# Layer 3 of a four-layer network: the four products that norm a chunk's tokens, spread over the slot schedule

## The chip, the cores and the metric

The kernel runs on one core of one Trainium2 chip. The metric is the device time of one execution in microseconds; the median over several executions is compared. The engines are TensorE (PE), VectorE (DVE), ScalarE (ACT), GpSimd (POOL) and SyncE (SP), which here issues nearly all DMAs.

## The reference

Four layers work in turn on an image batch of shape 8 x 64 x 64 x 64 in float32. The change touches the last layer, a bidirectional selective scan (Mamba) over the time axis and then over the frequency axis. Cut to what matters:

```python
def rms_norm(x, w):
    return x * lax.rsqrt(jnp.mean(x * x, axis=-1, keepdims=True) + EPS) * w

def mamba1(x, nw, ipw, cw, cb, xpw, dtw, dtb, Alog, Dp, opw):
    xn = rms_norm(x, nw)                       # the step that the change is about
    xc, z = split(xn @ ipw.T)
    xc = silu(causal_dwconv(xc, cw, cb))
    dt, Bm, Cm = from(xc @ xpw.T)              # dt = softplus(... )
    # h = h * exp(dt*A) + (dt*xc) * B ;  y = sum over 16 states of h * C
    y = selective_scan(xc, dt, Bm, Cm, -exp(Alog)) + Dp * xc
    return (y * silu(z)) @ opw.T

# time axis: directions 0 and 1; then frequency axis: directions 2 and 3
xt = mamba_bidir(xt, P, 0, 1) @ tlin_w + tlin_b + xt
xf = mamba_bidir(xf, P, 2, 3) @ flin_w + flin_b + xf
```

## The kernel before

**Stages, chunks, steps, slots.** `l3_stage` runs twice, once for each axis. A stage is 16 chunks of 2048 tokens (64 channels each). A chunk is eight steps: four groups `g` of 512 tokens, each in two directions `k` (0 forward, 1 backward). In this document the steps of a chunk are numbered 0 to 7, so odd steps are backward ones. A step works on tiles of 128 x 1024 and takes 16 slots, one for each state `n`. `stream` runs 2048 slots a stage, in one loop over `i`; the order of the program in a slot is the order in which each engine gets its instructions, since everything stands under a manual schedule.

**What a slot does.** For slot `i`, in this order:
- SP: `fetch(i+6)` loads the B and C rows of the state, broadcast to 128 partitions (line 1966, tile `bc`, 8 buffers). The load waits for the buffer that it goes into.
- POOL: `multiply_b(i+3)` makes `hb` (line 465, 4 buffers); and, if slot `i-1` is a *shared* one, `multiply_c(i-1)` on POOL (line 495, tile `h`). Shared slots are n = 1, 4, 7, 10, 13 in even steps and n = 2, 6, 10, 14 in odd ones.
- PE: `gather(i-2)` adds a state's `hc` (or `h`) into the step's sum `acc` (line 287). At n = 2 of a step the first gather of the new step comes after the slot's scan, and ahead of it stands `drain`.
- One piece of the next step's `prepare`, and one call of `advance` (below).
- DVE: `scan(i)` (line 481); `drain` of the step before, at n = 2 (line 1975, `z<-acc,z`: it reads the finished sum from PE); then `multiply_c(i)` on DVE (line 495, tile `hc`), unless the slot is shared.
- ACT: `decay(i+2)` (line 472, tile `dA`).

**The side work.** `begin(c+1)`, which fetches and norms the next chunk's tokens, is a generator in the queue `behind`; `finish`, which projects a finished group and adds the residual, is one in the queue `urgent`. `advance` runs one piece a slot. `urgent` goes first: while a `finish` is pending, and waits for a calm slot or for room in PSUM, nothing of `behind` moves. A `yield` of `CALM` or `CALM_FREE` makes the next piece wait for a slot in which neither it nor the one after is shared.

**begin**, in pieces: load of `raw`; squares on ACT, a mean on PE, `ms` to the small tile `rs` by DMA (twice); the root on ACT (line 1860); the reciprocal on DVE (line 1862); `rs` to a row in HBM (line 1865); two broadcasts of that row into `inv` (line 1869, 512 KB each, in pieces of 64 values); then four products `xn = raw * inv` on POOL (line 1877, 128 x 560 each), which `prepare` of the next chunk's steps reads. Counting the pieces through `advance` for a chunk in the middle of a stage gives these places, written (step, n): root (3, 3), reciprocal (3, 4), row (3, 5), `inv` (3, 7), the products (3, 9), (3, 10), (3, 11), (3, 12). A `finish` of two steps earlier holds `urgent` from n = 3 to n = 14 of every even step. The next chunk's first `prepare` starts at (7, 1).

`begin` stands beside the stream 15 times in each stage, 30 times in all; the first chunk's `begin` runs alone ahead of each stage.

Of the kernel before, what the change touches and what calls it, by code (L numbers as in the profile page):

```python
# [249 lines left out]
class Net:  # L250
# [1518 lines left out]
    def l3_stage(self, s, src, dst):  # L1769
# [6 lines left out]
        with ExitStack() as ctx:  # L1776
# [56 lines left out]
            def begin(c):  # L1833

                b, part = divmod(c, 2)
                q, rows = b // 2, slice((b % 2) * C, (b % 2) * C + C)
                x = raw[c % 2]
                hold = chunks[c] = {"x": x}
                from_ = src[q, rows, part * 4 * W : (part + 1) * 4 * W].rearrange("p (s t) -> p s t", t=HW)
                for r in range(2):  # L1840
                    nc.sync.dma_start(x[r * C : r * C + C, :, ends[r]], from_)
                yield False
                yield False
                rs = p1.tile([128, 16], F32, name="rs")
                for j in range(2):
                    yield CALM_FREE
                    sq = p1.tile([C, T], F32, name="sq")
                    o = sq.rearrange("p (s t) -> p s t", t=HW)
                    nc.scalar.activation(o, x[:C, j * 2 * H : (j + 1) * 2 * H, ends[0]], AF.Square)
                    yield  # L1850
                    ps = pp.tile([128, T], F32, name="mm")
                    self.mm(ps[:1, :], mean, sq)
                    yield CALM
                    ms = p1.tile([1, T], F32, name="ms")
                    nc.scalar.copy(ms, ps[:1, :])
                    yield False
                    nc.sync.dma_start(rs[j * 64 : j * 64 + 64], ms.rearrange("o (p e) -> o p e", e=16))
                yield False
                yield CALM_FREE
                nc.scalar.activation(rs, rs, AF.Sqrt, bias=self.eps5)  # L1860
                yield False
                nc.vector.reciprocal(rs, rs)
                yield False
                row = hp.tile([1, 4 * W], F32, name="rs")
                nc.sync.dma_start(row.rearrange("o (p e) -> (o p) e", e=16), rs)
                yield False
                yield False
                for r in range(2):
                    nc.sync.dma_start(
                        inv[r * C : r * C + C, :, ends[r]], row.rearrange("o (s t) -> o s t", t=HW).to_broadcast([C, 4 * H, HW])  # L1870
                    )
                yield False
                yield False
                hold["xn"] = p2.tile([128, 4 * H, HW + 6], F32, name="xn")
                for g in range(4):
                    at = slice(g * H, g * H + H)
                    nc.gpsimd.tensor_tensor(hold["xn"][:, at], x[:, at], inv[:, at], ALU.mult)  # L1877
                    yield False

            behind = deque()  # L1880
            begun = {}
# [2 lines left out]
            class Step:  # L1884
# [93 lines left out]
                def done(self):  # L1978
                    c, g = self.c, self.g
                    if self.k == 1:  # L1980
                        net.urgent.append(Task(finish(c, g, [chunks[c]["y0"], chunks[c]["y1"]])))
                    if self.k == 0 and g == 0 and c + 1 < 2 * NB:
                        begun[c + 1] = Task(begin(c + 1))
                        behind.append(begun[c + 1])
# [29 lines left out]
            with tc.manual_schedule():  # L2014
                Task(begin(0)).run()
                steps = [Step(c, g, k) for c in range(2 * NB) for g in range(4) for k in range(2)]
                self.stream(pools, (6, 3, 6), steps, behind)
# [26 lines left out]
```

## Time and profile before

| what | value |
|---|---|
| median of 3 runs | 25221.08 us |
| lowest, highest | 25216.33, 25233.35 us |
| the profiled execution | 25231.76 us |
| its span, first to last instruction | 25229.9 us |
| slots of layer 3, first to last scan | 11806 to 18470 us and 18547 to 25215 us |
| mean granted TensorE clock | 0.930 |

The span stands on the profile's page; the times of instructions are counted from its start. The profiled execution is 10.7 us longer than the median. Layer 3's two streams are 13332 us of the span, 53%. A line of the timeline has the start (us), the duration (us), engine, line, operation, tiles (out<-in), shape, count, and in brackets the idle time of the engine before it with what ended it.

### The profile page before, as it was taken

To read this page: it belongs to the slowest core of one execution; us is meant where nothing else is said; L and a number is where in the kernel's file an instruction comes from. 1 tells how busy PE (TensorE), PEld (TensorE's weight loads), DVE (VectorE), ACT (ScalarE), POOL (GpSimd) and SP (SyncE) were. 2 spreads that over 40 slices of the span, in tenths; PEclk is the share of its full clock that TensorE was granted. 3 is DMA by queue.
4 is the path that set the end of the run, shared out by engine and by line. 5 is a ranking of instruction groups with operands and counts; after the bars stand their busy time and mean duration, and the time that the engine had idled before them with its cause. 6 is when DMAs were issued, how large, how long until landed. Compare 5 with 4: busy or idle time off the path is not lost. (4 is left out here: it accounts for less than half of the span.)

```text
span 25229.9 us, 193412 instructions
## 1 busy us (share of the span) xinstructions
PE 21360.9 (85%) x53146; PEld 8333.8 (33%) x53146; DVE 22529.7 (89%) x13020; ACT 14745.3 (58%) x18562; POOL 22031.7 (87%) x10775
## 2 busy tenths in 40 slices
PE   8777888888888888888888888888878888888888
PEld 5522333333333323322333333333323333333333
DVE  4379989989989769978999999999989999999999
ACT  4344555555555455524666666666656666666666
POOL 0089999999999759976999999999989999999999
PEclk9888999999999999989999999999989999999999
DMA  2279898889898758842555555555545555555554
GB/s 60 77 279 321 310 317 311 311 313 316 307 315 311 251 194 323 324 134 79 167 170 169 171 166 171 169 170 167 167 155 169 168 170 168 170 168 171 167 171 157
DMA packets 1772400, 5282.72 MB, mean 209 GB/s; under 512 B 536352, under 2 KB 542564, under 8 KB 1703472
## 3 DMA queue, kind: packets, MB, share of 16 engines
q1 hardware_dynamic: 1744176, 5207.00, 61.0%
q10 hardware_dynamic: 27136, 63.34, 0.8%
q8 instruction: 423, 6.93, 0.1%
q14 instruction: 665, 5.45, 0.1%
HBM read 5112.85 MB, written 156.11 MB: 209 GB/s over the span
## 5 line engine op out<-in xcount | busy, mean ns | idle before, releaser
L465 POOL TENSOR_TENSOR hb<-du,bc 128x1024 f32<-128x1024 f32 x4608 | 10749.6, 2357 | 495.7 <-DVE h L481 334.4
L287 PE MATMUL acc<-hc,ident 128*128 128x512 f32 x18816 | 8878.8, 613 | 85.8 <-DVE img L1228 55.9
L472 ACT ACTIVATE dA<-dt,w_A 128x512 f32<-128x512 f32 x8192 | 5662.8, 691 | 4111.9 <-DVE hc L495 3125.9
L481 DVE TENSOR_TENSOR_SCAN dA<-dA,hb 128x1024 f32<-128x1024 f32 x3384 | 7726.0, 2283 | 282.5 <-ACT dA L472 118.4
L287 PE MATMUL acc<-h,ident 128*128 128x512 f32 x7808 | 4553.3, 713 | 2368.4 <-POOL h L495 2368.3
L287 PEld LDWEIGHTS acc<-hc,ident 128*128 128x128 f32 x18816 | 3689.4, 200 | 5292.2 <-issue 4656.8
L465 POOL TENSOR_TENSOR hb<-du,b 128x1024 f32<-128x1024 f32 x2048 | 4869.0, 2402 | 495.0 <-DVE h L481 253.7
L495 DVE TENSOR_TENSOR hc<-dA,bc 128x1024 f32<-128x1024 f32 x3296 | 4034.2, 1224 | 260.8 <-issue 8.9
L472 ACT ACTIVATE dA<-dt,w_l_A 128x1024 f32<-128x1024 f32 x2560 | 2856.5, 1117 | 1187.5 <-DVE hc L495 761.8
L481 DVE TENSOR_TENSOR_SCAN dA<-dA,carry,hb 128x1024 f32<-128x1024 f32 x1320 | 3093.9, 2344 | 172.9 <-ACT carry L1211 111.0
L287 PEld LDWEIGHTS acc<-h,ident 128*128 128x128 f32 x7808 | 1546.1, 215 | 5028.1 <-POOL h L495 3162.1
L481 DVE TENSOR_TENSOR_SCAN h<-dA,hb 128x1024 f32<-128x1024 f32 x1352 | 3081.5, 2279 | 46.0 <-ACT dA L472 40.3
L495 POOL TENSOR_TENSOR h<-h,bc 128x1024 f32<-128x1024 f32 x1312 | 3090.1, 2355 | 14.2 <-DVE h L481 14.2
L495 DVE TENSOR_TENSOR hc<-dA,c 128x1024 f32<-128x1024 f32 x1408 | 1722.5, 1223 | 115.6 <-DMA c<-bc 4.6
L495 POOL TENSOR_TENSOR h<-h,c 128x1024 f32<-128x1024 f32 x640 | 1511.9, 2362 | 8.6 <-ACT carry L1211 8.1
L481 DVE TENSOR_TENSOR_SCAN h<-dA,carry,hb 128x1024 f32<-128x1024 f32 x600 | 1404.4, 2341 | 77.9 <-ACT dA L472 71.6
L472 ACT ACT_TABLE_LOAD x1122 | 1439.5, 1283 | 21.1 <-ACT tmp L997 1.2
L1211 ACT COPY carry<-dA 128x1 f32<-128x1 f32 x1056 | 167.9, 159 | 1735.9 <-DVE hc L495 1674.0
L1911 PE MATMUL mm<-xn,taps 128*128 128x512 f32 x2048 | 937.9, 600 | 34.6 <-POOL xn L1877 32.3
L694 POOL MEMSET xf<- 128x24 f32 x33 | 4.3, 142 | 910.7 <-PE ps L715 731.3
L1926 PE MATMUL mm<-u,w_xp 128*36 128x512 f32 x1024 | 519.1, 632 | 140.5 <-ACT u L1923 135.4
L1946 POOL TENSOR_TENSOR du<-dt,u 128x1024 f32<-128x1024 f32 x256 | 601.4, 2349 | 18.7 <-ACT dt L396 18.7
(310 smaller groups left out, 18613.5 us busy)
## 6 DMA issues: line engine op xcount, KB each, us to landing
bc<-bc SPq DMA_DIRECT2D x4096, 512.0 KB
b<-bc SPq DMA_DIRECT2D x2048, 512.0 KB
c<-bc SPq DMA_DIRECT2D x2048, 512.0 KB
bc<-bc SPq DMA_DIRECT2D x512, 1024.0 KB
tmp<-rs SPq DMA_DIRECT2D x93, 512.0 KB
raw<-x SPq DMA_DIRECT2D x64, 512.0 KB
inv<-rs SPq DMA_DIRECT2D x64, 512.0 KB
tmp<-x SPq DMA_DIRECT2D x192, 128.0 KB
```

The lines of the kernel that those rows point to most:

```text
L287: self.nc.tensor.matmul(o, lhsT, r, start=start, stop=stop)
L465: nc.gpsimd.tensor_tensor(s.shaped(hb[i]), s.shaped(s.du), B.pop(i), ALU.mult)
L472: nc.scalar.activation(dA[i][:, cut], s.dt[:, cut], AF.Exp, scale=A[:, n : n + 1])
L481: nc.vector.tensor_tensor_scan(h[:, way], dA[i][:, way], hb.pop(i)[:, way], s.first(n), ALU.mult, ALU.add)
L495: engine.tensor_tensor(s.shaped(o), s.shaped(h), CC.pop(i), ALU.mult)
L694: nc.gpsimd.memset(x[:, :, HW:], 0.0)
L1211: nc.scalar.copy(self.carry[:, n : n + 1], h[:, last : last + 1])
L1911: nc.tensor.matmul(tokens(px[:, j * W : j * W + W]), taps[k][:, m, j * 128 : j * 128 + 128], xn[:, :, f : f + HW], start=m == 0, stop=m == 1,)
L1926: nc.tensor.matmul(pd, xp[:, k, j, :], u[:, j * W : j * W + W], start=j == 0, stop=j == 1)
L1946: nc.gpsimd.tensor_tensor(du, dt, u, ALU.mult)
```

## The change

One more empty piece stands between the root and the reciprocal, and eight more empty pieces stand between one product and the next. An empty piece costs one call of `advance`. Nothing else is changed.

```diff
                 nc.scalar.activation(rs, rs, AF.Sqrt, bias=self.eps5)
                 yield False
+                yield False
                 nc.vector.reciprocal(rs, rs)
                 yield False
                 row = hp.tile([1, 4 * W], F32, name="rs")
...
                 for g in range(4):
                     at = slice(g * H, g * H + H)
                     nc.gpsimd.tensor_tensor(hold["xn"][:, at], x[:, at], inv[:, at], ALU.mult)
-                    yield False
+
+                    for _ in range(9 if g < 3 else 1):
+                        yield False
```

Counted through `advance` in the same way, the places become: reciprocal (3, 5), row (3, 6), `inv` (3, 8), the products (3, 10), (4, 14), (5, 7), (6, 0). The gaps between the products are 20, 9 and 9 slots: the first gap holds the slots in which a pending `finish` keeps `behind` from moving.

## The prediction

> **What bounds the kernel now.** I read the waits of VectorE in layer 3 first (engine, line, what it waited for, total us, times, longest):
>
> ```profile
> DVE z L1975 <- PE acc L287: 159.1, 43, 5.6
> DVE dA L481 <- ACT dA L472: 70.7, 12, 34.0
> DVE rs L1862 <- ACT rs L1860: 49.4, 31, 16.7
> ...
> DVE dA L481 <- POOL hb L465: 4.8, 9, 2.0
> ```
>
> In the streams VectorE is nearly always running: the 70.7 us are mostly the starts of the stages. So a VectorE wait in a stream is time of the kernel, and two lines are left: the drain (L1975) and the reciprocal. Of the 159.1 us, by the rows of L1975, 144.1 us fall on the drain of step 3, in each of the 30 chunks with side work: 3.9 to 5.6 us, mean 4.81. The other drains wait 15 us in all. The windows of the two streams show a second engine as full (us, PE, PEld, DVE, ACT, POOL busy):
>
> ```profile
> 11806.00:18470.00 6664.00, 5723.76 (x11984) 2174.60 (x11982) 6446.78 (x3661) 4467.50 (x5772) 6457.36 (x2936) 0.95 0.52 168
> ```
>
> GpSimd is at 97%, with little to catch up with. The timeline of one chunk (GpSimd) shows the burst in step 3, the first and last of the four products, and the shared product n = 14 that closes the step, late:
>
> ```profile
> 14072.94 2.34 POOL L495 TENSOR_TENSOR h<-h,bc 128x1024 f32<-128x1024 f32 x1
> 14075.24 2.35 POOL L465 TENSOR_TENSOR hb<-du,bc 128x1024 f32<-128x1024 f32 x1
> 14077.55 2.34 POOL L1946 TENSOR_TENSOR du<-dt,u 128x1024 f32<-128x1024 f32 x1
> ...
> 14080.05 2.36 POOL L465 TENSOR_TENSOR hb<-du,bc 128x1024 f32<-128x1024 f32 x1
> 14082.45 1.37 POOL L1877 TENSOR_TENSOR xn<-raw,inv 128x560 f32<-128x560 f32 x1
> ...
> 14095.65 1.38 POOL L1877 TENSOR_TENSOR xn<-raw,inv 128x560 f32<-128x560 f32 x1
> ...
> 14103.90 2.36 POOL L495 TENSOR_TENSOR h<-h,bc 128x1024 f32<-128x1024 f32 x1
> ```
>
> TensorE and VectorE behind it, in the same chunk, then TensorE at the ends of steps 5 and 7 for comparison:
>
> ```profile
> 14106.32 3.78 PE L287 MATMUL acc<-h,ident 128*128 128x512 f32 x4 [4.51 <-POOL h L495]
> 14109.89 2.41 PE L287 MATMUL acc<-hc,ident 128*128 128x512 f32 x4
> ```
>
> ```profile
> 14061.17 0.25 DVE L1862 RECIPROCAL rs<-rs 128x16 f32<-128x16 f32 x1 [1.09 <-ACT rs L1860]
> ...
> 14112.33 1.23 DVE L1975 TENSOR_TENSOR z<-acc,z 128x1024 f32<-128x1024 f32 x1 [4.89 <-PE acc L287]
> ```
>
> ```profile
> 14208.61 2.51 PE L287 MATMUL acc<-h,ident 128*128 128x512 f32 x4 [3.23 <-POOL h L495]
> 14210.91 3.09 PE L287 MATMUL acc<-hc,ident 128*128 128x512 f32 x4
> ```
>
> ```profile
> 14311.16 1.98 PE L287 MATMUL acc<-h,ident 128*128 128x512 f32 x4 [1.50 <-POOL h L495]
> 14312.98 1.88 PE L287 MATMUL acc<-hc,ident 128*128 128x512 f32 x4
> ```
>
> The chain is: shared product 14 on GpSimd, eight matmuls, drain. In odd steps without a burst that product ends 6.54 us before VectorE is ready to drain (median of steps 5 and 7). The eight matmuls need 3.75 us after it when TensorE waited briefly, 5.45 in the slower of those steps, and 6.03 (median) in step 3. The burst makes the product 4 x 1.33 = 5.3 us later (1.33 is the pitch, 14082.45 to 14083.78). Then 6.03 + 5.3 - 6.54 = 4.8 us, the wait that is seen. Nothing of the 5.3 is caught up between, since GpSimd's idle gaps in odd steps lie at n = 5 to 7; from n = 8 on there is none.
>
> **The change part by part.**
>
> *The reciprocal, one slot later.* VectorE waits 1.09 us for the root, in each chunk (32.7 us over 30). A slot of 3.5 us more covers it. But the root and two table loads also delay ScalarE: the decay for the slot after is done at 14063.86, and the next scan, moved up by 1.09 from 14064.75, would want it at 14063.66. It waits some 0.2. Gain 0.9 us a chunk; between 0 and 1.1.
>
> *The row and the broadcast, one slot later on SP's queue.* This is the part that costs. SP works in order:
>
> ```profile
> 14066.20 0.35 SPq L1865 DMA_DIRECT2D rs<-rs  x1
> 14066.66 2.04 SPq L1966 DMA_DIRECT2D bc<-bc  x2
> 14069.89 4.65 SPq L1869 DMA_DIRECT2D inv<-rs  x2
> 14075.31 31.78 SPq L1966 DMA_DIRECT2D bc<-bc  x11
> ```
>
> The load at 14075.31 is slot 8's, and it waits for the buffer that shared product n = 6 on GpSimd frees (14072.94 + 2.34 = 14075.28). In the trace slot 8 of odd steps waits so in nearly every chunk. Now `inv` is issued ahead of that load; after the change it stands behind it, so not 3.5 us later but 5.8: at 14075.28 + 0.42 = 14075.70. The first product needs `inv`: from that product's end to it GpSimd has two `hb` more, a `du` and, with the slot added, a third `hb`: 9.5 us, so it is due at 14084.75. From the issue of `inv` to the start of its first reader the trace has 12.5 to 14.5 us in the seven chunks with a marked wait, and in the others last packet plus the 1.5 us that those show: 10 to 12.6, median of all about 11.5. One load ahead of it instead of two takes off perhaps 0.5; I take 11. GpSimd then waits 0.42 + 11 - 9.5 = 1.9 us in the first product's slot, where before the median wait is nil. The ends are 0 and 5.4 (at 14.5). Queued behind it are three `hb` and shared products 10 and 14, and TensorE's sums behind those.
>
> *Product 1, alone at (3, 10).* Product 14 of step 3 is later by 1.33 + 1.9 = 3.2 us instead of 5.3. TensorE's wait before it stays long, so 6.03 us is the nearest row for the matmuls: drain wait 6.03 + 3.2 - 6.54 = 2.7, and with rounding 2.8. Gain 2.0 us a chunk. With no wait for `inv` it would be 5.45 + 1.33 - 6.54 = 0.25, with 5.4 it would be 6.3.
>
> *Product 2 at (4, 14).* In slot 14 it comes behind shared product 13, the last of its step, so no drain stands behind it. Its 1.33 us is taken up by step 5's idle, 0.63 + 1.19 us before n = 6 and 7. Cost 0; without that cover it would be added to product 3.
>
> *Product 3 at (5, 7)* comes behind that idle and is not caught up: product 14 of step 5 is 1.33 us later. Its drain has 6.54 - 1.33 = 5.2 us for the matmuls: nothing lost at 3.75, 0.25 at 5.45, 0.8 at 6.03. TensorE's wait there, 1.3 to 3.2 us now, becomes 2.7 to 4.5, so rather the slow rows: 0.4. The Trainium skill, "TensorE: Matmul & The Clock Gate", section "What's actually happening", has the array fall to half clock after about 3.4 us of idle; the row with 3.23 us of idle above is already partly slow, so by the trace the limit lies somewhat lower. By the page half of these drains would stay quick and the sum would be some 6 us better.
>
> *Product 4 at (6, 0)* is behind step 5's last shared product. With what product 3 left and 0.67 us of idle in step 6, GpSimd is 2.0 us late at that step's end; the drain has 8.9 us from product 13 on and needs 5.5 to 7.1. Cost 0.1, up to 0.6. Step 7 has 2.1 us of idle for the rest. The first `prepare` that reads the products starts at (7, 1), 17 slots later.
>
> *The empty pieces* cost nothing on an engine, and `begin` ends long before the next chunk needs it.
>
> **The sum**, a chunk: 2.0 (drain 3) + 0.9 (reciprocal) - 0.4 (drain 5) - 0.1 (drain 6) = 2.4 us; times 30 = 72 us. The profiled execution of 25231.76 would be 25160; it lies 10.7 above the median, so 25149, 0.29% below 25221.
>
> **The rivals.** *A, the broadcast is in time.* If slot 8's load gets a buffer that VectorE frees, or the broadcast takes under 9.1 us with fewer loads beside it, drain 3 waits 0.25: (4.56 + 0.9 - 0.5) x 30 = 149 us, 25072. For it: packets alone take 7 to 10 us. Against: nearly all chunks show that buffer, and no broadcast was readable earlier than about 10 us.
>
> *B, a new wait for the old one.* The broadcast takes about 13.4 us, as in the chunks with a marked wait. GpSimd waits 4.3 us, drain 3 waits 5.2, and 4.81 - 5.2 + 0.9 - 0.5 = 0: 25221. For it: those seven rows. Against: they had two loads ahead.
>
> *C, slower.* Same place, but the broadcast loses its bandwidth to the loads of slots 8 to 11, which now follow it or go with it rather than being held. From 13.4 us it costs time; from 15.1 us (1.67 us a chunk more, 50 us) it can be measured; at 16.5 it is 3.1 x 30 = 93 us, 25314. Against: the longest of 30 is 14.5, and the bc loads are just as dense there.
>
> *D, the spread doesn't come about as counted*: product 2 directly nine slots on, at (4, 3). It would fall ahead of step 4's idle, 0.4 to 0.7 us, and change the sum by under 10 us; it is inside the forecast.
>
> **How the numbers follow.** Some 0.2%, 50 us, is what a measurement of this kernel tells from no change. Forecast with D 0.50, of which 0.10 gains under 50 us (broadcast over 11.8 us); A 0.20; B 0.20; C 0.10. Faster 0.40 + 0.20, same 0.10 + 0.20, slower 0.10. The range goes from A, 25070, to just above B, 25225, and leaves out C and the tail of A.
>
> **What would show it.** In the profile after: L1877 first in step 3, with a GpSimd wait for `inv` of about 2 us in most chunks (some 60 us in all; none would be A, over 120 B or C); SP's `inv` right behind a `bc` load that waited for POOL L495; the reciprocal's wait gone; drain waits of about 2.8 us at step 3 and 0 to 0.8 at step 5. A drain wait over 1 us at step 5 or 6, or a scan that waits for `hb`, would prove the lag arithmetic wrong.

## The result, and the profile after

| | before | after |
|---|---|---|
| median of 5 runs | 25221.08 us | 25129.41 us |
| lowest, highest | 25213.87, 25233.35 us | 25125.93, 25136.76 us |
| ratio, 95% interval | | 0.9963 [0.9951, 0.9975] |
| profiled execution | 25231.76 us | 25126.08 us |
| layer 3's streams, first to last scan | 6664.2 + 6668.4 us | 6623.3 + 6621.0 us |

The median fell by 92 us, 0.36%; 72 were forecast, and 25129 lies inside the range of 25070 to 25225. The streams of layer 3 are 88.3 us shorter. (The profiled executions differ by 105.7 us; the other 17.4 lie ahead of layer 3's first scan, where nothing was changed: that point falls between 11788.7 and 11807.4 us in the ten profiles of this study.)

VectorE's waits in layer 3, after (what waited, for what, total us, times, longest):

```profile
DVE z L1978 <- PE acc L287: 58.7, 73, 3.9
DVE h L481 <- ACT dA L472: 43.8, 55, 0.8
DVE dA L481 <- ACT dA L472: 40.6, 32, 31.9
DVE rs L1863 <- ACT rs L1860: 17.1, 1, 17.1
```

The drains (now L1978) wait 58.7 us instead of 159.1; the reciprocal no longer waits in a stream (the 17.1 us are one wait ahead of the second stage). The second line is new: it had 2.9 us before.

GpSimd in the same chunk of the first stage as was shown before, from shared product 6 of step 3 to shared product 14:

```profile
14042.95 2.35 POOL L495 TENSOR_TENSOR h<-h,bc 128x1024 f32<-128x1024 f32 x1
...
14050.08 4.68 POOL L465 TENSOR_TENSOR hb<-du,bc 128x1024 f32<-128x1024 f32 x2
14056.13 1.37 POOL L1878 TENSOR_TENSOR xn<-raw,inv 128x560 f32<-128x560 f32 x1 [1.37 <-DMA inv<-rs]
...
14071.29 2.36 POOL L495 TENSOR_TENSOR h<-h,bc 128x1024 f32<-128x1024 f32 x1
```

SP's queue there:

```profile
14038.40 7.25 SPq L1969 DMA_DIRECT2D bc<-bc  x2
14045.74 3.23 SPq L1870 DMA_DIRECT2D inv<-rs  x2
```

The broadcast stands behind the load that shared product 6 releases: that product ends at 14045.30, `inv` is issued at 14045.74, the first product is due at 14054.76 and starts at 14056.13, 10.4 us after the issue. Over layer 3 GpSimd's waits for `inv` are these, after:

```profile
POOL xn L1878 <- DMA inv<-rs: 95.5, 31, 40.0
```

One of the 31 is the 40.0 us ahead of the second stage; the other 30, one in each chunk, are 55.5 us, 1.85 each. Before, the 30 chunks had 6.0 in all.

TensorE at the end of step 3, which had 6.03 us of matmuls before:

```profile
14073.71 1.98 PE L287 MATMUL acc<-h,ident 128*128 128x512 f32 x4 [2.56 <-POOL h L495]
14075.53 1.88 PE L287 MATMUL acc<-hc,ident 128*128 128x512 f32 x4
```

Both groups are quick now, 3.7 us together, and this chunk's drain follows at 14077.44 without a marked wait. Over the 30 chunks the drain of step 3 waits 0.59 us instead of 4.80.

The new wait, in step 7 of the same chunk; TensorE, then ScalarE, then VectorE:

```profile
14226.12 3.59 PE L287 MATMUL acc<-h,ident 128*128 128x512 f32 x4 [3.48 <-POOL h L495]
14229.50 3.73 PE L287 MATMUL acc<-hc,ident 128*128 128x512 f32 x8
14233.07 3.67 PE L1914 MATMUL mm<-xn,taps 128*128 128x512 f32 x8
```

```profile
14236.77 1.26 ACT L1926 ACTIVATE u<-mm,w_cb 128x512 f32<-128x512 f32 x2 [1.99 <-PE mm L1914]
...
14243.76 0.58 ACT L1932 COPY dbl<-mm 36x512 f32<-36x512 f32 x1 [2.99 <-PE mm L1929]
14244.24 2.75 ACT L472 ACTIVATE dA<-dt,w_A 128x512 f32<-128x512 f32 x4
```

```profile
14233.27 1.23 DVE L1978 TENSOR_TENSOR z<-acc,z 128x1024 f32<-128x1024 f32 x1 [1.24 <-PE acc L287]
...
14245.75 2.29 DVE L481 TENSOR_TENSOR_SCAN h<-dA,hb 128x1024 f32<-128x1024 f32 x1 [0.81 <-ACT dA L472]
```

Shared product 13 of step 6 is late. Its sums hold the drain (1.24 us) and, on TensorE's queue, the first matmuls of the next `prepare` (L1914). So `u` is late on ScalarE, and so are the matmuls of `dbl` and its copy; on ScalarE's queue the decay stands behind that copy, and the scan at (7, 6) waits 0.81 us for it. A scan eight slots on in the schedule pays for a GpSimd product that it does not read.

### The profile page after: what moved, and what is told of

Read it like the earlier page. It is cut to its first block, busy times and chain, and to the rows that moved or that the text cites. A ratio compares the mean times of both kernels' runs of the same rounds, so it can differ in the third digit from the quotient of the medians.

```text
span 25124.3 us, 193472 instructions
## 1 busy us (share of the span) xinstructions
PE 21234.8 (85%) x53146; PEld 8296.4 (33%) x53146; DVE 22526.0 (90%) x13020; ACT 14730.3 (59%) x18562; POOL 22026.1 (88%) x10775
## 5 line engine op out<-in xcount | busy, mean ns | idle before, releaser
L1914 PE MATMUL mm<-xn,taps 128*128 128x512 f32 x2048 | 937.3, 599 | 34.5 <-POOL xn L1878 32.3
```

What stands on the lines that cost most here:

```text
L1914: nc.tensor.matmul(tokens(px[:, j * W : j * W + W]), taps[k][:, m, j * 128 : j * 128 + 128], xn[:, :, f : f + HW], start=m == 0, stop=m == 1,)
```

## The experiments

All kernels below are edits of the changed kernel, but for the one before idle time without the root slot, which is an edit of the kernel before. T and R in the expectations are the theory and its rival. Each was timed in five rounds against the kernel before, whose medians were 25224.31 us in the first four and 25223.44 us in the last four comparisons. The intervals reach some 0.12% (30 us) to either side; differences between these kernels that are smaller rest on the spread of the runs, 8 to 28 us from lowest to highest, and on the waits in the profiles.

| kernel | places of reciprocal, `inv`, products | median us | ratio, 95% interval |
|---|---|---|---|
| changed | (3,5), (3,8); (3,10), (4,14), (5,7), (6,0) | 25129.41 | 0.9963 [0.9951, 0.9975] |
| root slot only | (3,5), (3,8); (3,10) to (3,13) | 25247.96 | 1.0009 [1.0, 1.0018] |
| spread only | (3,4), (3,7); (3,9), (4,2), (5,6), (5,15) | 25102.65 | 0.9951 [0.9939, 0.9964] |
| broadcast a slot earlier | (3,5), (3,7); (3,10), (4,14), (5,7), (6,0) | 25076.30 | 0.9941 [0.9928, 0.9953] |
| products before idle time | (3,5), (3,8); (4,14), (5,2), (6,14), (6,15) | 25046.05 | 0.9928 [0.9916, 0.9941] |
| burst before idle time | (3,5), (3,8); (4,14), (4,15), (5,0), (5,1) | 25091.98 | 0.9950 [0.9937, 0.9962] |
| burst, broadcast in time | (3,5), (3,7); (3,10) to (3,13) | 25193.64 | 0.9989 [0.9980, 0.9998] |
| before idle time, no root slot | (3,4), (3,7); (4,14), (5,2), (6,14), (6,15) | 25071.28 | 0.9942 [0.9929, 0.9954] |
| fourth product late | (3,5), (3,8); (3,10), (4,14), (5,7), (6,14) | 25085.09 | 0.9948 [0.9935, 0.9960] |

**The root slot alone.**

```diff
-                    for _ in range(9 if g < 3 else 1):
-                        yield False
+                    yield False
```

> Only the extra slot between root and reciprocal; the four products stay back to back, now at (3, 10) to (3, 13). Theory T (the broadcast falls behind slot 8's load, and what GpSimd is late by reaches the drain): GpSimd waits about 1.9 us a chunk for inv, the burst adds 5.3 us, so shared product 14 of step 3 is 7.2 us late instead of 5.3 and the drain of step 3 waits about 6.7 us instead of 4.8, less if scans wait for hb first. The reciprocal gains 0.8. Together about +1 us a chunk, some 30 us slower than the kernel before: 25250 us. Rival R (GpSimd's wait for inv is harmless, the parts simply add up): the reciprocal's 0.9 us a chunk is gained, 25194 us, and the drain of step 3 waits 4.8 us as before.

Measured: 25247.96 us. VectorE's drains with the root slot alone:

```profile
DVE z L1977 <- PE acc L287: 186.3, 40, 6.8
```

GpSimd waits 96.0 us for `inv`, 40.2 of it ahead of the second stage. So it waits 1.86 us a chunk, as in the changed kernel (1.85), and behind a burst this lateness goes on to the drain: step 3's waits 5.85 us instead of 4.80. T expected 6.7 or less; part of the rest shows as scans waiting for `hb` (11.2 us, before 4.8). R is out: the parts don't add up by themselves, one half of the change loses 24 us (the interval just touches no change).

**The spread alone.**

```diff
                 nc.scalar.activation(rs, rs, AF.Sqrt, bias=self.eps5)
                 yield False
-                yield False
                 nc.vector.reciprocal(rs, rs)
```

> Only the empty pieces between the products; the reciprocal stays at (3, 4), the broadcast at (3, 7), ahead of slot 8's load; the products come at (3, 9), (4, 2), (5, 6), (5, 15). T: the reciprocal waits 1.09 us in each chunk again (33 us in all), GpSimd waits for inv hardly more than in the kernel before (under 10 us in 30 chunks), the drain of step 3 waits for nothing. Against the changed kernel: +33 for the reciprocal, -18 for the drain of step 3, -8 for the scan at (3, 5), up to -20 for the scan at (5, 6): 25115 to 25140 us. R: 27 us slower than the changed kernel, 25156.

Measured: 25102.65 us, 27 us below the changed kernel and 12 below T's lower end. GpSimd waits 6.4 us for `inv` in 30 chunks, the reciprocal 32.6 again, step 3's drain 3.4. T named the places of product 2, (4, 2), and product 4, (5, 15), but had not counted what they change: less is left for step 6, whose drain waits for nothing (19.7 us in the changed kernel), and the scan at (7, 6) too. The scan at (5, 6), for which T allowed up to 20 us, gains nothing: it waits 21.0 us. R, 25156, is out.

**The broadcast one slot earlier, the products where they are.**

```diff
                 nc.vector.reciprocal(rs, rs)
-                yield False
                 row = hp.tile([1, 4 * W], F32, name="rs")
...
                 yield False
                 yield False
+                yield False
                 hold["xn"] = p2.tile([128, 4 * H, HW + 6], F32, name="xn")
```

> As the changed kernel, but the row goes out in the reciprocal's slot and the broadcast at (3, 7), ahead of slot 8's load; an empty piece ahead of the products keeps them at (3, 10), (4, 14), (5, 7), (6, 0). T: GpSimd's wait for inv (55 us over 30 chunks in the changed kernel) is gone; then the drain of step 3 (17.6 us) and of step 4 (4.4 us) wait for nothing and the scan at (5, 6) (0.65 us a chunk) waits less; the drain of step 6 and the scan at (7, 6) stay, since they hang on products 3 and 4. Gain 25 to 40 us against the changed kernel: 25090 to 25105 us. R: GpSimd has idle time anyway, nothing changes: 25129 us.

Measured: 25076.30 us, 53 us below the changed kernel. GpSimd's wait for `inv` here:

```profile
POOL xn L1878 <- DMA inv<-rs: 42.8, 4, 40.3
```

Less the 40.3 ahead of the second stage, 2.5 us are left of 55.5. Only the row and its broadcast were moved, and the time falls by about as much as that wait did (53 us by the medians, 58 by the streams of the profiled executions). This fits that GpSimd's lateness is paid somewhere, once the waits at step 3 do not let it catch up. T had the direction and the place; it expected 25 to 40, since it held that step 6 would not gain, and its drain went from 19.7 to 6.0 us.

**The products before idle time.**

```diff
+                for _ in range(9):
+                    yield False
                 hold["xn"] = p2.tile([128, 4 * H, HW + 6], F32, name="xn")
...
-                    for _ in range(9 if g < 3 else 1):
+                    for _ in range((4, 17, 1, 1)[g]):
                         yield False
```

> Reciprocal and broadcast as in the changed kernel, the products at (4, 14), (5, 2), (6, 14), (6, 15): each behind the last shared product of an even step and ahead of the idle time that GpSimd has at n = 5 to 7 of the odd step. T: what counts is the place against GpSimd's idle time and the last shared product of a step, not the distance. No wait for inv, no drain wait at steps 3, 4 and 6 (42 us gone), the scans at (5, 6) and (7, 6), late through the same sums on TensorE, wait less (up to 43 us gone); what stays is the reciprocal's gain. 25050 to 25080 us. R (distance counts; two pairs five and one slots apart are half a burst): drains of steps 5 and 7 wait 1 us or more, 25129 us or slower.

Measured: 25046.05 us, 178 us below the kernel before and 83 below the changed one: the fastest here. VectorE's waits:

```profile
DVE dA L481 <- ACT dA L472: 77.1, 40, 33.8
DVE z L1980 <- PE acc L287: 19.2, 17, 2.8
```

In the streams no drain but step 1's waits (13.7 us, as in the kernel before: 12.3), and the wait of `h` scans for ScalarE has dropped from 43.8 to 1.3 us. GpSimd's idle time before its `hb` in step 5 falls from 1.84 us (before) to 0.01, in step 7 from 2.10 to 0.01: the products stand where GpSimd would have waited. What is left are the stage starts, step 1's drain, and 0.28 us at (3, 5). Not all of the 83 us are the place's: at (4, 14) the first product no longer waits for `inv`, and that wait alone is worth 53 us by the run before. Against that run, in which the broadcast is in time too, the place is worth 30 us (25076.30 - 25046.05).

**Back to back, before idle time.**

```diff
+                for _ in range(9):
+                    yield False
                 hold["xn"] = p2.tile([128, 4 * H, HW + 6], F32, name="xn")
...
-                    for _ in range(9 if g < 3 else 1):
-                        yield False
+                    yield False
```

> Reciprocal and broadcast as in the changed kernel, the four products back to back again, but at (4, 14), (4, 15), (5, 0), (5, 1), behind the last shared product of step 4 and ahead of step 5's idle time. T: GpSimd enters step 5 5.3 us late and loses 1.9 us of that to its idle time; 3.4 us reach shared product 14 of step 5, so its drain has 3.1 us for matmuls that take 3.75: 0.6 us of wait (2.3 if TensorE is slow). Some 2 us then reach step 6 as they do in the changed kernel: drain of step 6 about 0.6, scan (7, 6) about 0.8. Some 2 us a chunk over the products before idle time (25046): 25108 us, at most 25150. R (back to back is what costs, wherever it stands): 4.8 us a chunk as in the kernel before, 25190 us.

Measured: 25091.98 us, 37 us faster than the changed kernel with its products spread. The waits in the chunks are step 5's drain, 0.94 us, step 6's, 0.12, and the scan at (7, 6), 0.51. VectorE, this kernel:

```profile
DVE z L1979 <- PE acc L287: 42.5, 46, 3.6
...
DVE h L481 <- ACT dA L472: 16.6, 22, 0.8
```

R is out. But the 37 us do not show that the place is worth more than the distance, since the later place also takes away the wait for `inv`: with the broadcast in time and the products where they were, the spread kernel is faster still (25076.30 us). Back to back is 46 us behind the products before idle time, which is what distance still gives; T said 62.

**A burst with the broadcast in time.** The edits of the broadcast one slot earlier and of the root slot alone together.

> The root slot with a burst at (3, 10) to (3, 13), as in the run with the root slot alone, but the row goes out in the reciprocal's slot and the broadcast at (3, 7), ahead of slot 8's load. T: GpSimd's wait for inv is gone, the drain of step 3 waits 4.8 us again instead of 5.85, and the reciprocal's gain is left: 25224 - 25 = 25200 us, 48 us under the root slot alone. R (the reciprocal's wait only moves elsewhere, and the root slot alone is slower for another reason): 25224 us or above.

Measured: 25193.64 us, 54 us under the root slot alone. GpSimd waits 1.8 us for `inv` in 30 chunks, step 3's drain 4.96 us. Against the kernel before, 30 us are gained: the reciprocal's 32.7 less the 8 that the scan at (3, 5) gives back would be 25, and the interval holds both. R is out. This run also gives the place's worth for a burst whose broadcast is in time: 102 us (25193.64 - 25091.98).

**Before idle time, without the root slot.** The products of the fastest kernel (with one empty piece more ahead of them), the reciprocal at (3, 4).

> The products at (4, 14), (5, 2), (6, 14), (6, 15), but the reciprocal at (3, 4) as in the kernel before. T: VectorE waits 1.09 us for the root in each chunk, 33 us, and the scan at (3, 5) no longer waits 0.28: 24 us above the 25046 of the products before idle time, 25070 us. R (VectorE's wait for the root gives GpSimd and TensorE time that they need anyway): no difference, 25046 us.

Measured: 25071.28 us, 25 above the fastest; VectorE waits 32.7 us for the root again (49.5, less 16.8 ahead of the second stage). R is out.

**The fourth product late.**

```diff
-                    for _ in range(9 if g < 3 else 1):
+                    for _ in range((9, 9, 12, 1)[g]):
```

> The changed kernel with the fourth product at (6, 14) in place of (6, 0), the others as they are. T: shared product 13 of step 6 is then late by what product 3 leaves only, under 0.7 us; the drain of step 6 (19.7 us over 30 chunks) and the scan at (7, 6) (24 us) wait for nothing, the waits in steps 3 to 5 stay: 25129 - 44 = 25085 us. R (the scans wait for ScalarE for a reason of its own): the drain goes, the scan at (7, 6) keeps its 0.8 us, 25110 us.

Measured: 25085.09 us, 44 us under the changed kernel. VectorE, this kernel:

```profile
DVE h L481 <- ACT dA L472: 20.7, 26, 0.8
```

One product moved by fourteen slots takes away step 6's drain wait (19.7 to 0.0 us) and the scan's at (7, 6) (one wait of 0.7 us is left; `h` scans wait 20.7 us for ScalarE instead of 43.8). The scan at (5, 6) keeps its 0.65 us, as it hangs on product 13 of step 4, still late by product 1 and the wait for `inv`. So ScalarE's lateness in step 7 is GpSimd's, passed on by TensorE. For step 5 the products before idle time show the same: there the scan at (5, 6) waits 0.6 us in all 30 chunks together. R is out.

**The parts, measured.** With the root slot and `inv` at either place the spread is worth 119 us (25247.96 - 25129.41) or 117 (25193.64 - 25076.30). The late broadcast costs 54 us (25247.96 - 25193.64) with a burst and 53 with the products spread. The reciprocal's wait is worth 30 us with a burst and 25 before idle time. -118 + 53 - 28 = -93 us; the change measures -92. The parts are less exact than they look: by the streams of the profiled executions the late broadcast costs 42 us with the burst and 58 with the products spread.

Place and distance, with no wait for `inv` in any of the four kernels: the place alone is worth 102 us for a burst, the distance alone 117 (25193.64 - 25076.30), both together 148 (25193.64 - 25046.05). The first two lie too close to be ranked, and either takes away most of what the other would.

## Why the prediction was right, and where its sizes were off

By its own steps, in us a chunk:

| step | forecast | measured |
|---|---|---|
| drain of step 3 | -2.0 | -4.21 (4.80 to 0.59) |
| reciprocal | -0.9 | -0.81 (1.09 less 0.28 at (3, 5)) |
| drain of step 5 | +0.4 | 0.0 |
| drain of step 6 | +0.1 | +0.66 |
| drain of step 4 | none | +0.15 |
| scans at (5, 6) and (7, 6) | none | +0.65, +0.80 |
| sum | -2.4 | -2.76 |

2.76 x 30 is 83 us of the 88.3 that the streams lost; the small rest was not traced. The direction and the path were forecast; that the sum came so near was in part luck. Over 30 chunks the drains of steps 3 and 5 gained 78 us more than forecast, and the other rows lost 68 us more.

*SP's queue* was right in each term. `inv` was forecast 0.42 us behind the end of shared product 6 and came 0.44 behind it; the first product was due 9.5 us after that end, and was; GpSimd's wait was forecast as 1.9 and is 1.85. From issue to reader the broadcast took 10.4 us in the chunk shown and 10.9 in the mean of the 30, and I took 11.

*The matmuls behind product 14 of step 3* are the term that was mis-sized: 6.03 us, taken from the burst's own rows, where 3.76 (median) came. I argued that TensorE's wait before that product stays long. It doesn't: the whole delay falls ahead of product 10, so TensorE stands still 7.5 us before that one (as it did before the change), where no drain follows, and the distance from product 10 to product 14 is that of an undisturbed step. In the burst two of the four products fell between them. TensorE's wait before product 14 is 2.54 us (median), 5.37 before the change. The runs agree: 5.97 us of wait went with 5.80 us of matmuls (root slot alone), 1.9 with 3.75 (broadcast a slot earlier). With 3.76 the step's own formula gives 3.76 + 3.2 - 6.54 = 0.4; 0.59 was measured. Step 5 went the same way: I took the slow rows, and its wait before product 14 is 2.6 us, its matmuls 3.76, its drain wait nil. At these two drains the bound that the Trainium skill states ("TensorE: Matmul & The Clock Gate", section "What's actually happening"), about 3.4 us of idle before the array slows, points to the quick rows, and 58 of these 60 groups were quick. As a bound the trace does not bear it out: at step 6 twelve matmuls took 7.1 us (median) behind a wait of 2.69 us before the change, and 7.17 behind 3.47 us after it, where the quick rows have 5.47. The limit does lie lower, as the prediction read from its row with 3.23 us; the last section has what the granted clock shows.

*What was given back* was missed in size. The drain wait of step 3 had one use: it let GpSimd catch up. Without it GpSimd enters step 4 still some 3 us late. Its idle time there, which I counted at 0.4 to 0.7 us, is 0.01, and step 5's 1.84 is 0.08, as it goes to what step 3 left; so products 3 and 4 find nothing to be taken up by, and step 6's product 13 is 2 us late as forecast (median). The drain pays 0.66 where 0.1 was forecast, 0.6 at most.

*The scans at (5, 6) and (7, 6)* were no step at all. I followed the late sums to the drain and not to the matmuls that stand behind them on TensorE's queue, and from there to ScalarE. That cost 1.45 us a chunk, 43 us, and hid most of the error in step 3.

Rival A's time was right for its condition: with the broadcast in time the changed kernel measures 148 us under the kernel before (25224.31 - 25076.30), 149 were worked out. A's sum had no term for the scans at (5, 6) and (7, 6), which still waited 25 us there, so the match is partly luck. B and C needed a broadcast of 13.4 us and more; it was quicker here. D did not occur: the places are those counted, 20, 9 and 9 slots apart. One of the signs that were to prove the lag arithmetic wrong did come: the drain of step 6 waited over 1 us in 14 of the 30 chunks. In five of them, the chunk shown among them, product 13 was 3 us late instead of 2, so there the lag was wrong; in the other nine it was 2 us late, and the matmuls took over 8 us where 7.1 was the most that was reckoned with. Step 5's drain did not wait, and scans waited 0.8 us in all for `hb`.

## What to carry to other kernels

Before side work is moved on a nearly full engine, list that engine's idle time slot by slot and the last instruction of each period that another engine's sum hangs on; side work belongs behind that instruction and ahead of the idle time. Spreading it out is no lesser means: the place alone was worth 102 us here, the distance alone 117, and both 148. Of a step moved by one slot, look at the DMAs that it issues and at what they now stand behind on their queue: one slot cost 5.8 us here, since a load held the queue. A wait that is removed was also time for others to catch up, so follow what they are late by to the next idle time, through every queue that it passes.

## What the runs showed of the hardware

A broadcast of 64-value pieces, twice 512 KB, took 10.0 to 12.2 us from its issue to its first reader with one load ahead of it (mean 10.9, changed kernel), so that a slot's distance to its reader decides whether it is covered.

TensorE's pace behind a wait did not follow from the length of the wait alone. Of 900 groups of eight matmuls at the ends of steps 3, 5 and 7 in the ten profiles, all 220 behind waits under 1.85 us took 3.7 us, 165 of 199 behind 1.85 to 2.25 us were slower, mostly 5.4 us, 354 of 361 behind 2.25 to 3.0 us were quick again, so were 19 of 21 behind 3.0 to 3.3 us, and all 99 behind more than 4 us took 5.1 to 6.7 us.

The record of the granted clock in the traces shows why. In layer 3's streams the clock changes only on a grid of 3.41 us, and it falls to half after a piece of that grid in which TensorE was busy for less than some four tenths (by the profile's busy times, in which the ends of matmuls are modelled). At full clock, over the ten profiles, 2337 of 2343 pieces with a busy share under 0.41 were followed by half clock, and 71 of 31890 with a share over 0.45. So some 2 us of standing still are enough, an estimate from these shares, if they fall into one piece. At the end of step 4 in the chunk shown, TensorE waited 2.80 us before the change, a piece of 3.40 us had 0.69 us of work, and the clock fell to 0.50; after the change it waited 3.48 us, but over two pieces with 1.73 and 1.59 us of work, and the clock stayed at 1.00.
